# Attention kernel on one core: scores and attention times v in phases per block, with norm and projections spread over blocks

## The chip, the cores and the metric

The kernel runs on one core of a Trainium2 chip. TensorE (PE) multiplies matrices into PSUM, ScalarE (ACT) evaluates functions, VectorE (DVE) and GpSimd (POOL) do elementwise work, SyncE (SP) issues the DMAs. The metric is the device time of one execution in microseconds (us), the median of several runs.

## The reference

The input x has the shape 16 x 256 x 32 x 32. Two layers of the same form follow one another; each adds to x an attention over the 1024 positions of an image, with four heads of 64 channels. All in float32.

```python
def layer(x, Wq, bq, Wk, bk, Wv, bv, rel_h, rel_w):        # x: 16, 256, 32, 32
    xf = gn(x).reshape(16, 256, 1024)     # gn: mean and variance over the channels, the first
                                          # space axis and pairs of the last axis: 16 groups
    q, k, v = (W @ xf + b, each as 16, 4, 64, 1024)
    rel  = (rel_h + rel_w).reshape(4, 64, 1024)
    attn = softmax(einsum('bhdi,bhdj->bhij', q, k) + einsum('hdi,bhdj->bhij', rel, q), -1)
    return x + einsum('bhdn,bhmn->bhdm', v, attn).reshape(x.shape)
```

## The kernel before

The work is cut into 32 *units*: one image in one layer. The images alternate, so that layer 1 of an image comes three units after its layer 0 (for the first image two). A unit has four *blocks*: two pairs of heads (pr), and for each two halves of 512 rows i. A block has eight *chunks* j of 128 columns of the softmax axis. The tiles of a block carry pr and half in their names: `ps_0_1_2` is the score tile of pair 0, half 1, chunk 2; the last number in the order listings only tells buffers apart.

`scores` makes one chunk for both heads of the pair: per head k times q, and two matmuls that add the position term from its two parts `hi` and `lo`. The head of 64 channels takes half of the rows of the array. The scores lie in a PSUM tile `ps`, of which there are three; every projection (`pq`, `pk`, `pv`), the position term `pa`, the group means `pm` and the denominators `pd` take tiles of the same three. ACT writes p = exp(ps - 36) to SBUF, and DVE adds the p of the eight chunks into `acc`. `attend` multiplies two chunks of p with v into `po`, half of the columns of the array per head; `po` lies in one of two PSUM tiles for the whole block.

The denominators (`denominators`): a matmul of acc with ones gives `pd`, ACT copies it to SBUF (`den`), and two DMAs put it across the partitions (`den_all`), so that DVE takes the reciprocal of 8 numbers per partition (L284). A DMA writes these to DRAM (`rd`), another reads them back, repeated for all partitions of a head (`rden`). I call this the trip. `finish` multiplies `po` by `rden` (L298) and adds bias and x (L299); in layer 1 an image's half is then written out (L301).

The work for the next unit is cut into slices, of which one goes behind each chunk from the second block on: the norm (DVE sums, PE averages over partitions, POOL subtracts, squares, takes the power -0.5 and multiplies: L128 to L140), and then the projections. `attend` follows two chunks behind the scores. The denominators of a block come behind the fourth chunk of the next block, and finish behind the eighth.

The order on each engine is not quite that of the text: a scheduler takes the instructions by their place in the text and by when it expects their operands and buffers, and lays down one list per engine, which the engine then works off in order.

## Time and profile before

| | |
|---|---|
| time, median of 3 runs | 3864.93 us (3862.89 to 3867.33) |
| profiled execution | 3863.41 us, span 3861.6 us |
| granted TensorE clock, mean over the span | 0.963 of 2.4 GHz |
| PE busy | 3538.8 us, 92% |
| PE weight loads (beside matmuls) | 1501.0 us, 39% |
| DVE busy | 1705.3 us, 44% |
| ACT busy | 1490.2 us, 39% |
| POOL busy | 676.1 us, 18% |
| DMA traffic | 72.33 MB, 19 GB/s |

A row of the groups by line shows: line, engine, operation, output <- inputs by the program's names, shapes, count | busy us in total, mean ns of one | idle us of the engine just before them, and what ended it. A row of a timeline shows: start in us, length in us, engine, line, operation, output <- inputs, number of instructions merged, and in brackets the idle time before it and what released it. A matmul in float32 shows as two instructions per operand pair; lengths of successive matmuls overlap, so the time that one costs is read from start to start. A row of the windows shows: window in us and its length, then busy us (and count) of PE, PE's weight loads, DVE, ACT and POOL, the granted clock, the share of the DMA engines' time and GB/s.

### The profile page before, as it was taken

How to read it: one execution, taken by the hardware profiler on the slowest of the kernel's cores; microseconds unless marked ns; L12 is line 12 of the kernel's file. 1: busy time of each engine (PE TensorE's matmuls, PEld its weight loads, DVE VectorE, ACT ScalarE, POOL GpSimd, SP SyncE). 2: the span in 40 equal slices, each digit the busy share in tenths (PEclk: the TensorE clock that was granted, in tenths of full speed). 3: DMA queues.
4: the chain of work that ended last, by engine and by line, in shares of the span. 5: the costliest groups of instructions: out<-in, count | busy, mean ns of one | idle time of the engine just before them, and what ended most of it. 6: DMA issues, size and time to landing. Idle time of an engine off the chain costs nothing.

```text
span 3861.6 us, 37025 instructions
## 1 busy us (share of the span) xinstructions
PE 3538.8 (92%) x15386; PEld 1501.0 (39%) x15386; DVE 1705.3 (44%) x1556; ACT 1490.2 (39%) x1409; POOL 676.1 (18%) x134
## 2 busy tenths in 40 slices
PE   6999999999989999999999989999999999999996
PEld 3433443334433334333344333443333433334432
DVE  2444444444434444344543344433355444454443
ACT  2333443344433344333344333443343433334433
POOL 2122111221112221122211122111222112221110
PEclk9999999999999999999999999999999999999998
DMA  1000000000000000000000000000000000000000
GB/s 51 9 9 17 25 9 14 27 16 26 9 15 27 15 27 8 17 25 15 28 9 31 9 15 27 9 31 9 17 25 11 29 11 15 25 18 14 9 15 31
DMA packets 69487, 72.33 MB, mean 19 GB/s; under 512 B 43200, under 2 KB 44736, under 8 KB 69312
## 3 DMA queue, kind: packets, MB, share of 16 engines
q1 hardware_dynamic: 69312, 69.90, 5.3%
q8 instruction: 122, 2.00, 0.2%
q14 instruction: 53, 0.43, 0.0%
HBM read 52.04 MB, written 17.30 MB: 18 GB/s over the span
## 4 chain that ended last, share of the span: by engine, by line
PE 53%; POOL 16%; DMA 16%; DVE 12%; issue 2%; SPq 1%; ACT 1%; DVEq 0%; POOLq 0%
PE ps L233 12%; DMA rden<-rd 12%; PE po L257 11%; PE pq L152 7%; PE pv L196 6%; PE pk L152 6%; PE ps L238 5%; POOL xc L128 4%; POOL rstd L139 4%; DVE acc L248 4%; POOL xc L140 4%; POOL sq L130 4%; PE pa L170 3%; DMA rd<-r 3%; DMA den_all<-den 2%; PE pd L276 2%
## 5 line engine op out<-in xcount | busy, mean ns | idle before, releaser
L242 ACT ACTIVATE p<-ps,shift 128x1024 f32<-128x1024 f32 x1024 | 1141.4, 1115 | 1006.3 <-PE ps L238 996.4
L248 DVE TENSOR_TENSOR acc<-acc,p 128x1024 f32<-128x1024 f32 x768 | 1121.0, 1460 | 603.5 <-ACT p L242 574.2
L257 PE MATMUL po<-p,v 128*64 128x512 f32 x4096 | 1036.2, 628 | 123.1 <-DVE o L298 123.1
L233 PE MATMUL ps<-q,k 64*128 64x512 f32 x4096 | 1132.2, 629 | 0.0
L238 PE MATMUL ps<-pick,hi 64*128 64x512 f32 x2048 | 826.4, 800 | 0.0
L128 POOL TENSOR_TENSOR xc<-x,mean 128x2048 f32<-128x2048 f32 x32 | 175.7, 5491 | 2432.9 <-DVE mean L126 2432.9
L233 PEld LDWEIGHTS ps<-q,k 64*128 64x128 f32 x4096 | 341.9, 187 | 493.4 <-issue 335.1
L257 PEld LDWEIGHTS po<-p,v 128*64 128x64 f32 x4096 | 255.4, 139 | 622.5 <-issue 479.2
L238 PE MATMUL ps<-pick,lo 64*128 64x512 f32 x2048 | 411.0, 393 | 0.0
L298 DVE TENSOR_TENSOR o<-po,rden 128x512 f32<-128x512 f32 x128 | 88.6, 692 | 701.4 <-DMA rden<-rd 656.0
L152 PE MATMUL pq<-xc,Wq 128*128 128x512 f32 x512 | 271.7, 680 | 108.0 <-POOL xc L140 108.0
L139 POOL TENSOR_TENSOR rstd<-var,mhalf 128x32 f32<-128x32 f32 x32 | 204.9, 6405 | 584.5 <-DVE var L135 584.5
L238 PEld LDWEIGHTS ps<-pick,hi 64*128 64x128 f32 x2048 | 200.3, 189 | 245.9 <-issue 245.9
L238 PEld LDWEIGHTS ps<-pick,lo 64*128 64x128 f32 x2048 | 199.7, 188 | 244.8 <-issue 244.8
L280 ACT COPY den<-pd 128x512 f32<-128x512 f32 x128 | 75.1, 587 | 437.6 <-PE pd L276 436.0
L196 PE MATMUL pv<-Wv,xc 128*128 128x256 f32 x1024 | 237.8, 385 | 0.0
L152 PE MATMUL pk<-xc,Wk 128*128 128x512 f32 x512 | 236.6, 605 | 0.0
L246 DVE TENSOR_TENSOR acc<-p,p 128x1024 f32<-128x1024 f32 x128 | 156.4, 1222 | 128.5 <-ACT p L242 128.5
L196 PEld LDWEIGHTS pv<-Wv,xc 128*128 128x128 f32 x1024 | 189.4, 190 | 60.2 <-ACT p L242 25.2
L152 PEld LDWEIGHTS pq<-xc,Wq 128*128 128x128 f32 x512 | 104.4, 214 | 260.5 <-issue 138.8
L180 DVE TENSOR_TENSOR lo<-pa,hi 128x1024 fp32r<-128x1024 f32 x64 | 78.4, 1224 | 283.2 <-ACT hi L179 282.8
L160 ACT ACTIVATE q<-pq,bq 128x1024 f32<-128x1024 f32 x64 | 71.3, 1115 | 340.2 <-PE pq L152 340.2
(57 smaller groups left out, 1322.6 us busy)
## 6 DMA issues: line engine op xcount, KB each, us to landing
rden<-rd SPq DMA_DIRECT2D x128, 256.0 KB
x<-in_x_dram SPq DMA_DIRECT2D x32, 512.0 KB
out_dram<-x SPq DMA_DIRECT2D x32, 512.0 KB
den_all<-den SPq DMA_DIRECT2D x256, 2.0 KB
rd<-r SPq DMA_DIRECT2D x128, 4.0 KB
wn0Wq<-in_L_conv_Wq_dram SPq DMA_DIRECT2D x1, 256.0 KB
wn0Wk<-in_L_conv_Wk_dram SPq DMA_DIRECT2D x1, 256.0 KB
wn0Wv<-in_L_conv_Wv_dram SPq DMA_DIRECT2D x1, 256.0 KB
```

The lines of the kernel that those rows point to most:

```text
L128: nc.gpsimd.tensor_tensor(rows(xc, H), rows(src, H), per_column(mean), ALU.subtract)
L130: nc.gpsimd.tensor_tensor(sq, xc, xc, ALU.mult)
L139: nc.gpsimd.tensor_tensor(rstd, var, W.mhalf, ALU.pow)
L140: nc.gpsimd.tensor_tensor(rows(xc, H), rows(xc, H), per_column(rstd), ALU.mult)
L152: nc.tensor.matmul(pk[:, nh, :], w[l][:, cc, pr * P : (pr + 1) * P], xns[u][:, cc, nh * HALF : (nh + 1) * HALF], start=(cc == 0), stop=(cc ...
L196: nc.tensor.matmul(pv[:, i, :], xns[u][:, cc, t * P : (t + 1) * P], W.wv[l][:, cc, :], start=(cc == 0), stop=(cc == CC - 1),)
L233: nc.tensor.matmul(ps[:, h, :], ks[u, pr][hs[h], jc], qs[u, pr][hs[h], ic], start=True, stop=False)
L238: nc.tensor.matmul(ps[:, h, :], part[u, pr][hs[h], jc], W.pick[hs[h], ic], start=False, stop=last)
L242: nc.scalar.activation(p, ps, AF.Exp, bias=W.shift)
L246: nc.vector.tensor_tensor(accs[blk], probs[blk, 0], p, ALU.add)
L248: nc.vector.tensor_tensor(accs[blk], accs[blk], p, ALU.add)
L257: nc.tensor.matmul(outs[blk][h * D : (h + 1) * D, :], vts[u][:, j, c0 : c0 + D], p[:, h, :], start=(j == 0), stop=(j == NT - 1),)
```

## The change

`attend` now runs once per block, over all eight chunks, and makes `pd` right behind; both `po` and `pd` take tiles of the pool of two, and ACT copies both to SBUF. `reciprocals` is the rest of the trip; it stands behind the fourth chunk of the next block, and `finish`, which reads the copy of po, behind the eighth. The norm is cut in four pieces and the projections in three groups, each at a fixed place: `before_block` runs ahead of the scores of a block, `norm_a` and `norm_c` behind them. The variance's power is taken on 16 columns instead of 32, and POOL spreads the result with a copy. The projections of q and k for the first pair of heads come a block early, in the last block of the unit before. There are 3 instead of 4 buffers for each of q, k, hi and lo, and 10 instead of 8 for p.

```diff
-    kqpool = ctx.enter_context(tc.tile_pool(name="kqpool", bufs=4))
+    kqpool = ctx.enter_context(tc.tile_pool(name="kqpool", bufs=3))
-    ppool = ctx.enter_context(tc.tile_pool(name="ppool", bufs=8))
+    ppool = ctx.enter_context(tc.tile_pool(name="ppool", bufs=10))
...
+    def norm_d(u):
+        xc = xns[u]
+        var = small.tile([P, G], F32, tag="var", name=f"var_{u}")
+        nc.vector.tensor_scalar(var, group_mean(u, "v"), EPS, None, ALU.add)
+        rstd = small.tile([P, G], F32, tag="rstd", name=f"rstd_{u}")
+        nc.gpsimd.tensor_tensor(rstd, var, W.mhalf[:, :G], ALU.pow)
+        rs = small.tile([P, H], F32, tag="rs", name=f"rs_{u}")
+        nc.gpsimd.tensor_copy(rs.rearrange("p (g t) -> p g t", t=GT), spread(rstd))
+        nc.gpsimd.tensor_tensor(rows(xc, H), rows(xc, H), per_column(rs), ALU.mult)
...
-    def attend(blk, j):
+    def attend(blk):
...
+        po = ps_o.tile([P, HALF], F32, tag="o", name=f"po_{name}")
+        for j in range(NT):
...
+        pd = ps_o.tile([P, HALF], F32, tag="o", name=f"pd_{name}")
...
+        outs[blk] = fpool.tile([P, HALF], F32, tag="ou", name=f"ou_{name}")
+        nc.scalar.copy(outs[blk], po)
...
-        o = fpool.tile([P, HALF], F32, tag="o", name=f"o_{u}_{pr}_{half}")
-        nc.vector.tensor_tensor(o, outs.pop(blk), rdens.pop(blk), ALU.mult)
+        o = outs.pop(blk)
+        nc.vector.tensor_tensor(o, o, rdens.pop(blk), ALU.mult)
...
+    def before_block(n):
+
+        u, b = divmod(n, BPU)
+        nxt = u + 1 if u + 1 < len(units) else None
+        if b == 0:
+            if u > 0:
+                positions(u, 0)
+            values(u, 0)
+            values(u, 1)
+        elif b == 1:
+            if nxt is not None:
+                norm_b(nxt)
+            project(u, 1, "q")
+            project(u, 1, "k")
+            positions(u, 1)
+        elif b == 2:
+            if nxt is not None:
+                norm_d(nxt)
+        elif nxt is not None:
+            project(nxt, 0, "q")
+            project(nxt, 0, "k")
...
+    for n, blk in enumerate(blocks):
+        before_block(n)
+        for j in range(NT):
+            scores(blk, j)
+            if n > 0 and j == 3:
+                reciprocals(blocks[n - 1])
+        if n > 0:
             finish(blocks[n - 1])
...
+            if b == 0:
+                norm_a(u + 1)
+                if u + 2 < len(units) and units[u + 2][1] == 0 and units[u + 2][0] > 1:
+                    load_x(units[u + 2][0])
+            elif b == 1:
+                norm_c(u + 1)
+        attend(blk)
```

PE, the end of the second block of unit 4, before (`ps` are scores, `po` attention times v):

```order
L233 MATMUL ps_0_1_6_2646<-q_0_2247,k_0_2271 128x512 x2
L238 MATMUL ps_0_1_6_2646<-pick,hi_0_2285 128x512 x2
L238 MATMUL ps_0_1_6_2646<-pick,lo_0_2286 128x512 x2
L233 MATMUL ps_0_1_7_2656<-q_0_2247,k_0_2271 128x512 x2
L238 MATMUL ps_0_1_7_2656<-pick,hi_0_2285 128x512 x2
L238 MATMUL ps_0_1_7_2656<-pick,lo_0_2286 128x512 x2
L257 MATMUL po_0_1_2604<-p_0_1_4_2629,v_2304 64x512 x2
L257 MATMUL po_0_1_2604<-p_0_1_5_2639,v_2304 64x512 x2
L233 MATMUL ps_1_0_0_2676<-q_1_2368,k_1_2385 128x512 x2
L238 MATMUL ps_1_0_0_2676<-pick,hi_1_2404 128x512 x2
```

and now, where the eight rows of po stand together, of which the first and the last are shown, and `pd` and the variance's `pm_v` follow:

```order
L231 MATMUL ps_0_1_7_2675<-q_0_2301,k_0_2308 128x512 x2
L236 MATMUL ps_0_1_7_2675<-pick,hi_0_2427 128x512 x2
L236 MATMUL ps_0_1_7_2675<-pick,lo_0_2428 128x512 x2
L257 MATMUL po_0_1_2690<-p_0_1_0_2606,v_2431 64x512 x2
...
L257 MATMUL po_0_1_2690<-p_0_1_7_2682,v_2431 64x512 x2
L267 MATMUL pd_0_1_2707<-acc_0_1_2617,ones 64x512 x2
L121 MATMUL pm_v_2717<-red_v_2687,avg 128x16 x2
L231 MATMUL ps_1_0_0_2726<-q_1_2583,k_1_2590 128x512 x2
```

Two chunks of scores and two of po took turns; now eight and eight do, with one change of form each way.

DVE in the second block of unit 4, before. `r_4_0_0` is the reciprocal for the block before it, `o` and `x` are the two operations of its finish, `red_v` sums the squares that POOL makes from `xc`:

```order
L246 TENSOR_TENSOR acc_0_1_2569<-p_0_1_0_2555,p_0_1_1_2567 128x1024
L126 COPY mean_2588<-pm_m_2585 128x32
L248 TENSOR_TENSOR acc_0_1_2569<-acc_0_1_2569,p_0_1_2_2582 128x1024
L248 TENSOR_TENSOR acc_0_1_2569<-acc_0_1_2569,p_0_1_3_2601 128x1024
L104 TENSOR_REDUCE red_v_2673<-sq_2592 128x16 x2
L104 TENSOR_REDUCE red_m_3100<-x_935 128x16 x2
L284 RECIPROCAL r_4_0_0_2616<-den_all 128x8
L248 TENSOR_TENSOR acc_0_1_2569<-acc_0_1_2569,p_0_1_4_2629 128x1024
L248 TENSOR_TENSOR acc_0_1_2569<-acc_0_1_2569,p_0_1_5_2639 128x1024
L298 TENSOR_TENSOR o_0_0_2670<-po_0_0_2479,rden_0_0_2620 128x512
L299 SCALAR_TENSOR_TENSOR x_206<-o_0_0_2670,bv_156,x_206 128x512
L248 TENSOR_TENSOR acc_0_1_2569<-acc_0_1_2569,p_0_1_6_2653 128x1024
```

and now, from the mean on, where `ou` is the copy of po, and `lo_1` is the second part of the position term of the next pair of heads:

```order
L140 COPY mean_2569<-pm_m_2570 128x32
L284 RECIPROCAL r_4_0_0_2639<-den_all 128x8
L109 TENSOR_REDUCE red_v_2687<-sq_2576 128x16 x2
L296 TENSOR_TENSOR ou_0_0_2563<-ou_0_0_2563,rden_0_0_2643 128x512
L297 SCALAR_TENSOR_TENSOR x_206<-ou_0_0_2563,bv_156,x_206 128x512
L196 TENSOR_TENSOR lo_1_2596<-pa_1_2592,hi_1_2595 128x1024
L244 TENSOR_TENSOR acc_0_1_2617<-p_0_1_0_2606,p_0_1_1_2615 128x1024
L246 TENSOR_TENSOR acc_0_1_2617<-acc_0_1_2617,p_0_1_2_2626 128x1024
```

The reciprocal and both operations of finish have moved ahead of all additions of the block, and so have red_v and lo_1.

DVE in the first block of unit 5, before:

```order
L246 TENSOR_TENSOR acc_0_0_2992<-p_0_0_0_2981,p_0_0_1_2990 128x1024
L248 TENSOR_TENSOR acc_0_0_2992<-acc_0_0_2992,p_0_0_2_3005 128x1024
L248 TENSOR_TENSOR acc_0_0_2992<-acc_0_0_2992,p_0_0_3_3015 128x1024
L284 RECIPROCAL r_4_1_1_3030<-den_all 128x8
L248 TENSOR_TENSOR acc_0_0_2992<-acc_0_0_2992,p_0_0_4_3043 128x1024
L248 TENSOR_TENSOR acc_0_0_2992<-acc_0_0_2992,p_0_0_5_3053 128x1024
L298 TENSOR_TENSOR o_1_1_3084<-po_1_1_2884,rden_1_1_3034 128x512
L299 SCALAR_TENSOR_TENSOR x_206<-o_1_1_3084,bv_156,x_206 128x512
L248 TENSOR_TENSOR acc_0_0_2992<-acc_0_0_2992,p_0_0_6_3067 128x1024
```

and now, where `x_3089` is the tile of an image that this block loads, for the norm of unit 7:

```order
L196 TENSOR_TENSOR lo_0_2973<-pa_0_2969,hi_0_2972 128x1024
L284 RECIPROCAL r_4_1_1_3037<-den_all 128x8
L296 TENSOR_TENSOR ou_1_1_2963<-ou_1_1_2963,rden_1_1_3041 128x512
L297 SCALAR_TENSOR_TENSOR x_206<-ou_1_1_2963,bv_156,x_206 128x512
L244 TENSOR_TENSOR acc_0_0_3015<-p_0_0_0_3004,p_0_0_1_3013 128x1024
L109 TENSOR_REDUCE red_m_3633<-x_3089 128x16
L246 TENSOR_TENSOR acc_0_0_3015<-acc_0_0_3015,p_0_0_2_3024 128x1024
L109 TENSOR_REDUCE red_m_3633<-x_3089 128x16
L246 TENSOR_TENSOR acc_0_0_3015<-acc_0_0_3015,p_0_0_3_3034 128x1024
```

The reciprocal and finish stand ahead of the first addition, and the two sums of the new image between the first additions. In the third block the same two operations follow the first addition; in the fourth they stand ahead of all.

## Rows read from the trace of the kernel before

**Rows 1.** Groups of instructions by line, six lines out of all
```profile
L257 PE MATMUL po<-p,v 128*64 128x512 f32 x4096 | 1036.2, 628 | 123.1 <-DVE o L298 123.1
...
L152 PE MATMUL pq<-xc,Wq 128*128 128x512 f32 x512 | 271.7, 680 | 108.0 <-POOL xc L140 108.0
...
L139 POOL TENSOR_TENSOR rstd<-var,mhalf 128x32 f32<-128x32 f32 x32 | 204.9, 6405 | 584.5 <-DVE var L135 584.5
...
L140 POOL TENSOR_TENSOR xc<-xc,rstd 128x2048 f32<-128x2048 f32 x32 | 152.8, 4774 | 2.5
...
L280 ACT COPY den<-pd 128x512 f32<-128x512 f32 x128 | 75.1, 587 | 437.6 <-PE pd L276 436.0 <-DMA x<-in_x_dram 1.6
...
L114 PE MATMUL pm_m<-red_m,avg 128*128 128x16 f32 x128 | 20.4, 271 | 6.2 <-DVE red_m L104 6.2
```

**Rows 2.** Timeline of PE, one undisturbed pair and two pauses
```profile
1016.76 1.94 PE L257 MATMUL po<-p,v 128*64 128x512 f32 x8
...
1089.15 5.40 PE L152 MATMUL pq<-xc,Wq 128*128 128x512 f32 x8 [3.90 <-POOL xc L140]
...
2857.37 2.84 PE L257 MATMUL po<-p,v 128*64 128x512 f32 x8 [2.92 <-DVE o L298]
```

**Rows 3.** Timeline of PE at the start
```profile
51.10 3.60 PE L152 MATMUL pk<-xc,Wk 128*128 128x512 f32 x8
54.53 1.88 PE L170 MATMUL pa<-q,rel 128*128 128x512 f32 x4
56.25 7.07 PE L196 MATMUL pv<-Wv,xc 128*128 128x256 f32 x32
...
71.83 1.13 PE L233 MATMUL ps<-q,k 64*128 64x512 f32 x4
...
73.27 1.02 PE L233 MATMUL ps<-q,k 64*128 64x512 f32 x4
...
74.58 1.03 PE L233 MATMUL ps<-q,k 64*128 64x512 f32 x4
```

**Rows 4.** Timeline of all engines, the last block
```profile
3825.59 3.65 PE L257 MATMUL po<-p,v 128*64 128x512 f32 x16
...
3834.26 1.81 PE L276 MATMUL pd<-acc,ones 128*64 128x512 f32 x4 [5.01 <-DVE acc L248]
...
3839.07 0.20 DVE L284 RECIPROCAL r<-den_all 128x8 f32<-128x8 f32 x1 [4.96 <-DMA den_all<-den]
...
3848.07 0.69 DVE L298 TENSOR_TENSOR o<-po,rden 128x512 f32<-128x512 f32 x1 [8.80 <-DMA rden<-rd]
```

**Rows 5.** Timeline of PE and DVE, the longest trip to DRAM
```profile
403.44 1.03 PE L276 MATMUL pd<-acc,ones 128*64 128x512 f32 x4
...
418.32 0.69 DVE L298 TENSOR_TENSOR o<-po,rden 128x512 f32<-128x512 f32 x1 [6.29 <-DMA rden<-rd]
```

**Rows 6.** Timeline of DVE, mid-run
```profile
1134.07 0.69 DVE L298 TENSOR_TENSOR o<-po,rden 128x512 f32<-128x512 f32 x1 [5.01 <-DMA rden<-rd]
...
1135.47 1.22 DVE L248 TENSOR_TENSOR acc<-acc,p 128x1024 f32<-128x1024 f32 x1
1136.67 1.23 DVE L180 TENSOR_TENSOR lo<-pa,hi 128x1024 fp32r<-128x1024 f32 x1
...
1167.96 0.18 DVE L126 COPY mean<-pm_m 128x32 f32<-128x32 f32 x1
...
1169.54 5.32 DVE L248 TENSOR_TENSOR acc<-acc,p 128x1024 f32<-128x1024 f32 x1 [0.16 <-ACT p L242]
1178.35 2.35 DVE L104 TENSOR_REDUCE red_v<-sq 128x16 f32<-128x1024 f32 x2 [3.49 <-POOL sq L130]
```

**Rows 7.** Timeline of the SP queue, a write of x and the next load
```profile
1164.47 0.34 SPq L301 DMA_DIRECT2D out_dram<-x  x1
1167.49 0.82 SPq L86 DMA_DIRECT2D x<-in_x_dram  x2
```

**Rows 8.** Busy time by window, the end of that load
```profile
1171.00:1171.50 0.50, 0.50 (x4) 0.30 (x4) 0.50 (x1) 0.38 (x1) 0.50 (x1) 1.00 0.63 254
```

More of the change, by code (lines that the diff above doesn't have):

```diff
@@ L66, in fast_path @@
     NL = sh.NL
-    LAG = 2
     xpool = ctx.enter_context(tc.tile_pool(name="xpool", bufs=3))
@@ L99, in psum2, with reduce_groups @@
         return ps_s.tile([P, 2, HALF], F32, tag="s", name=name)
-    def group_mean(src, name):
-        red = small.tile([P, CC, G], F32, tag="red", name=f"red_{name}")
+    reds = {}
+    def reduce_groups(u, src, what):
+        red = small.tile([P, CC, G], F32, tag=f"red_{what}", name=f"red_{what}_{u}")
         for cc in range(CC):
@@ L109, in group_mean @@
             )
-        yield
-        yield
-        pm = psum2(f"pm_{name}")
+        reds[u, what] = red
+    def group_mean(u, what):
+        red = reds.pop((u, what))
+        pm = psum2(f"pm_{what}_{u}")
         for cc in range(CC):
@@ L130, in norm_slices, with norm_c @@
         nc.gpsimd.tensor_tensor(sq, xc, xc, ALU.mult)
-        for _ in range(5):
-            yield
-        pv = yield from group_mean(sq, f"v{u}")
-        var = small.tile([P, H], F32, tag="var", name=f"var_{u}")
-        nc.vector.tensor_scalar(
-            var.rearrange("p (g t) -> p g t", t=GT), pv, EPS, None, ALU.add
-        )
-        rstd = small.tile([P, H], F32, tag="rstd", name=f"rstd_{u}")
-        nc.gpsimd.tensor_tensor(rstd, var, W.mhalf, ALU.pow)
-        nc.gpsimd.tensor_tensor(rows(xc, H), rows(xc, H), per_column(rstd), ALU.mult)
-        xns[u] = xc
-        for _ in range(5):
-            yield
+        xns[u], sqs[u] = xc, sq
+    def norm_c(u):
+        reduce_groups(u, sqs.pop(u), "v")
+    def norm_d(u):
[7 more added lines that the diff above has]
+        nc.gpsimd.tensor_tensor(rows(xc, H), rows(xc, H), per_column(rs), ALU.mult)
     def project(u, pr, which):
@@ L301, in finish @@
             nc.sync.dma_start(flat(out[b, pr * P : (pr + 1) * P]), xt[b][:, pr, :])
-    for f in (norm_slices, projection_slices):
-        for _ in f(0):
-            pass
     blocks = [(u, pr, half) for u in range(len(units)) for pr in range(CC) for half in range(NH)]
@@ L310, in fast_path @@
         index[blk] = n
-    steps = [(blk, j) for blk in blocks for j in range(NT)]
-    BPU = CC * NH * NT
-    prep = iter(())
-    for g in range(len(steps) + LAG):
-        if g < len(steps):
-            scores(*steps[g])
-        if g % 2 == 1:
-            for a in (g - LAG - 1, g - LAG):
-                if 0 <= a < len(steps):
-                    attend(*steps[a])
-        n, c = divmod(g, NT)
-        if c == LAG + 1 and n > 0:
-            rdens[blocks[n - 1]] = denominators(blocks[n - 1])
-        if c == NT - 1 and n > 0:
+    BPU = CC * NH
+    def before_block(n):
[18 more added lines that the diff above has]
+            project(nxt, 0, "k")
+    for f in (norm_a, norm_b, norm_c, norm_d):
+        f(0)
+    project(0, 0, "q")
+    project(0, 0, "k")
+    positions(0, 0)
+    for n, blk in enumerate(blocks):
[5 more added lines that the diff above has]
+        if n > 0:
             finish(blocks[n - 1])
-        u, step = divmod(g, BPU)
-        if g < len(steps):
-            if step == NT:
+        u, b = divmod(n, BPU)
+        if u + 1 < len(units):
+            if b == 0:
+                norm_a(u + 1)
                 if u + 2 < len(units) and units[u + 2][1] == 0 and units[u + 2][0] > 1:
                     load_x(units[u + 2][0])
-                if u + 1 < len(units):
-                    prep = chain(norm_slices(u + 1), projection_slices(u + 1))
-            next(prep, None)
-    blk = blocks[-1]
-    for a in range(len(steps) - LAG, len(steps)):
-        if (steps[a][0], steps[a][1]) in probs:
-            attend(*steps[a])
-    rdens[blk] = denominators(blk)
-    finish(blk)
+            elif b == 1:
+                norm_c(u + 1)
+        attend(blk)
+    reciprocals(blocks[-1])
+    finish(blocks[-1])
 @with_exitstack
```

75 lines of the change are left out of this document (28 added, 47 removed).

## The prediction

> **What bounds the kernel now.** I read the share of each engine first, then the list of groups by line, then the timelines of PE, DVE and SP around one unit, and last how the change orders PE and DVE. PE is the engine that is busy nearly all the time; what it loses are drains and two pauses in each unit. In the list of groups [rows 1] the reader is to see the idle time ahead of two lines: 123.1 us before attention times v (L257), which waits for DVE's product o because o still holds the PSUM tile, and 108.0 us before the q projection (L152), which waits for POOL's normalised xc. The PE timeline shows what these pauses also do to the clock [rows 2]: after 3.90 us of pause eight projection matmuls take 5.40 us, against 3.60 us for the same eight in [rows 3]; after 2.92 us eight matmuls of po take 2.84 instead of 1.94 us. I read both as stretches at the lower of the clock's two levels, 1.2 instead of 2.4 GHz, behind a pause. I take the first one's 5.40 - 3.60 = 1.8 us per pause of two to four us.
>
> A unit of before takes (3836.07 - 71.83) / 32 = 117.6 us, from the first score [rows 3] to the end of the last pd [rows 4].
>
> **The change on PE.** The matmuls are the same; what goes are switches between forms. At the start, where four chunks of scores stand in a row, the first lasts 1.44 us to the start of the next and the second 1.31 [rows 3]; so eight chunks take 1.44 + 7 x 1.31 = 10.61 us. Attention times v for two chunks lasts 1.94 us, for four 3.65 [rows 2, 4], so each further pair 1.71 and all eight 1.94 + 3 x 1.71 = 7.07. pd takes 1.03 [rows 5]; q or k 3.43 and pa 1.72 from start to start, both halves of v 7.07 [rows 3]; a group mean 20.4 / 32 = 0.64 [rows 1]. At full clock, without waits:
> - first block (pa, v): 1.72 + 7.07 + 10.61 + 7.07 + 1.03 = 27.5 us
> - second (mean, q, k, pa): 0.64 + 3.43 + 3.43 + 1.72 + 18.71 = 27.9 us
> - third (variance): 0.64 + 18.71 = 19.35 us
> - fourth (next q, k): 6.86 + 18.71 = 25.6 us
>
> Together 100.35 us. If that were all, the change would take off a seventh.
>
> **The change on DVE.** Here the order decides. In the text the reciprocal follows the fourth chunk and finish the eighth; in DVE's queue both stand ahead of nearly all additions of the block, and everything behind waits for the reciprocal's trip through DRAM. I count from T, the end of the preceding block's pd. The last block of before shows the trip undisturbed: pd ends at 3836.07, the reciprocal starts 3.00 us later, the product 12.00 us later [rows 4]. The longest trip that I found lasts 418.32 - 404.47 = 13.85 us [rows 5]. I take 12.0, and keep 13.85 for the range. Product and addition to x take 1.40 us, an addition 1.22, lo 1.23 [rows 6].
>
> Third block: the variance, the reciprocal and the first addition are done early. The product comes at T + 12.0, six additions end at 12.0 + 1.4 + 6 x 1.22 = 20.7, while PE wants pd at 0.64 + 10.61 + 7.07 = 18.3. PE waits 2.4 us.
>
> Second block: the reduce of sq stands ahead of the product, and lo behind it. The mean starts at T + 0.74; the reduce starts 10.39 us after the mean, since POOL makes xc and sq in between, and takes 2.35 [rows 6], so it ends at 13.5; product and x end at 14.9, lo at 16.1. The third chunk of scores needs the PSUM tile that lo reads: with three tiles, the mean's goes to pa, and pa's to this chunk. PE is there at 9.22 + 1.44 + 1.31 = 12.0 and waits 4.1 us. The additions end well before pd.
>
> Fourth block: the additions end at 12.0 + 1.4 + 7 x 1.22 = 21.9; PE comes at 24.5. No wait, 2.6 us of cover. First block: lo comes first, behind pa (1.72) and ACT's cast of pa (a us, estimated from den's copy of half the size, 0.587 [rows 1]); so the reciprocal starts at 4.0 and the product, 9.0 behind it [rows 4], at 13.0; with one reduce of x the additions end at 24.1, and PE comes at 26.5. The cover is 2.4 us.
>
> Thirteen units (every odd one from 3 to 27) are heavier. Their first block has two reduces of an x that is only then loaded, among the additions. The load waits for the write of the x before it in its buffer: SP issues it 3.02 us after that write [rows 7], and its transfer ends 4.0 us after the issue [rows 8]. So: finish ends at T + 14.4, load issued at 17.4, halves there at about 20.0 and 21.4 (half of the megabyte each), reduce, addition, reduce, five additions end at 29.7. PE waits 3.2 us. Their third block has one reduce more: 21.9 instead of 20.7, and PE waits 3.6.
>
> **Other edits.** The copy of po is like den's, 0.587 us [rows 1]; ACT makes it while PE does pd, so it costs nothing; wholly in the way it would add 0.6 us to the trip. It frees PSUM early, and the 123.1 us go. The pow on half the columns and the new copy on POOL lie between nothing (pow at zero) and 6.4 us for the pow, with the multiplication's 4.8 behind it [rows 1]; even with a us for the copy xc is ready by T + 13 of the third block, and the q projection that wants it comes at T + 21.7. So the 108.0 us go as well. Fewer buffers for q and k and more for p: by the order nothing waits for them.
>
> The product now reads two operands in SBUF. The Trainium skill (SBUF — State Buffer, Who interferes with whom) says that a VectorE instruction with two SBUF inputs contends with a GpSimd instruction that reads SBUF, and that the one that starts second is held for all of the other. The trace agrees for an addition beside POOL's xc: 5.32 us instead of 1.22 [rows 6]. By that rule the product of the third block, beside POOL's multiplication, could be held to T + 13 at the latest, which adds up to 1 us to that block; by the forecast it is not held, since the multiplication ends before T + 12.
>
> **The sum.** A light unit: 100.35 + 4.1 + 2.4 + 2 x 1.8 = 110.5 us. A heavy one: 100.35 + 4.1 + 3.6 + 3.2 + 3.6 + 1.0 = 115.9 us; the last 1.0 is its pd at half clock, and the rest of that fall lies under the next wait. Start to the first score: 71.83 - 3.43 - 3.43 - 1.72 = 63.2. First unit: 110.5 - 8.8 (pa and v are in the start) = 101.7. Then 17 light units 1878.5 and 13 heavy ones 1506.7. Last unit, without a norm: lo ends at 14.6, and its third and fourth block end with the additions and pd at 21.7: 27.5 + 30.6 + 21.7 + 21.7 + three falls 5.4 = 107. End as before, 3861.6 - 3836.1 = 25.5. Sum 3682.6 us of span. The profiled execution of before took 1.8 us more than its span, and the median of the runs 1.5 us more than it: 3686 us, 4.6% less.
>
> **Rivals.**
> - The reciprocal is held by POOL. In the second block it falls beside xc. No row has it there. An addition that came late beside xc could begin only 5.68 us after the mean (1169.54 + 5.32 - 1.22 - 1167.96, [rows 6]). Then it starts at T + 6.4, the product at 15.4, lo ends at 18.0: 1.9 us more in 31 units, 3746 us. For it: additions are held. Against it: it has one small operand. The page of the Trainium skill named above says that an instruction with at most one SBUF input, outside the two-port modes, is not held; by it this rival falls; no row can show it.
> - The clock stays up after these waits, which are mostly shorter than 4 us: 18 x 3.6 + 13 x 4.6 + 5 = 130 us less, 3556 us. Against it: the row after 2.92 us.
> - The phases do not bring what I read: every chunk costs 1.44 and every pair of po 1.87. That is 1.3 us a block where PE sets the end: about 3.7 us in a light and 2.4 in a heavy unit, 98 us, 3784 us. Against it: the second and third chunk of [rows 3].
> - The waits in DVE's queue are all covered: 100.35 us a unit, 3286 us. Against it: the trip's 12.0 us, and the end of before [rows 4], where pd already sits 5.01 us behind such a product.
> - Slower: DVE's queue becomes the loop that sets the time, because the trip lasts longer where each block starts one. Four us more (16.0) cost 1.7 + 2.5 + 4.0 + 1.4 us in the blocks of a light unit and two further falls of the clock, 13.2 us, and 13.7 in a heavy one: 415 us, 4101 us. It decides from 2.8 us more (14.8) on, where the 5.8 us that a unit has gained are gone. For it: one trip of 13.85 us. Against it: the chain has no new step but the copy.
>
> **How the numbers follow.** Forecast 0.56; reciprocal held 0.17; clock up 0.08; phases without gain 0.05; all covered 0.03; trip longer 0.11. The forecast's own range is 3670 to 3780: a trip of 13.85 us costs some 92 us, and downwards half of the falls behind the 2.4 us waits may stay out (18 x 1.8 / 2 = 16 us). The range of 3550 to 3800 takes in the reciprocal, the clock and the phases, and leaves out the last two. About 0.2% is what a measurement can tell from no change. All cases but the long trip are faster by more: 0.89; of the long trip 0.02 falls near its turning point, and 0.09 is slower.
>
> **What would show it.** Right: PE's longest waits are for lo ahead of the third chunk in the second block, about 4 us, 31 times, and for the additions ahead of pd in the third block, 2 to 4 us, and in 13 first blocks; DVE's longest total is the product's wait for rden, 7 to 9 us each; a score chunk in a row takes 1.31 us; no pause before po or before the next unit's q. Wrong: pauses in first or fourth blocks of light units (a longer trip), a reciprocal that ends with xc, matmuls at full clock behind the waits, or chunks of 1.4 us.

## The result, and the profile after

The changed kernel takes 3642.28 us in the median of four runs (3635.63 to 3650.66), the one before took 3863.91 us beside it (3855.39 to 3867.33): ratio 0.9431, interval 0.9403 to 0.9458. The forecast was 3686 us, in a range of 3550 to 3800. The profiled execution took 3650.66 us, its span 3648.8 us, at a mean granted clock of 0.959.

The groups by line of the kernel after, which answer to [rows 1]; the columns are the same:

```profile
L231 PE MATMUL ps<-q,k 64*128 64x512 f32 x4096 | 1077.8, 601 | 57.2 <-DVE lo L196 57.2
...
L257 PE MATMUL po<-p,v 128*64 128x512 f32 x4096 | 907.1, 595 | 0.0
...
L168 PE MATMUL pq<-xc,Wq 128*128 128x512 f32 x512 | 308.8, 758 | 8.1 <-POOL xc L158 8.1
...
L267 PE MATMUL pd<-acc,ones 128*64 128x512 f32 x512 | 163.8, 724 | 177.8 <-DVE acc L246 177.8
...
L142 POOL TENSOR_TENSOR xc<-x,mean 128x2048 f32<-128x2048 f32 x32 | 144.3, 4510 | 2250.9 <-DVE mean L140 2250.9
...
L144 POOL TENSOR_TENSOR sq<-xc 128x2048 f32<-128x2048 f32 x32 | 115.2, 3599 | 2.5
...
L155 POOL TENSOR_TENSOR rstd<-var,mhalf 128x16 f32<-128x16 f32 x32 | 92.8, 2900 | 710.6 <-DVE var L153 710.6
L296 DVE TENSOR_TENSOR ou<-ou,rden 128x512 f32<-128x512 f32 x128 | 88.6, 692 | 666.8 <-DMA rden<-rd 640.4 <-ACT p L240 26.2
```

Both old pauses are gone: nothing is idle ahead of po (L257; 123.1 us before), and 8.1 us ahead of q (L168; 108.0 before), which is the very first normalisation. po takes 907.1 us of PE in place of 1036.2. Two new waits stand in their place: 57.2 us ahead of scores (L231), for lo, and 177.8 us ahead of pd (L267), for the additions. DVE's idle time ahead of the product (L296), until rden has come, is 640.4 us, 5.0 us each on average: 8.7 us in first and fourth blocks, 2.5 in third and 0.5 in second ones, where the prediction's sign had 7 to 9 us each.

PE in a light unit, second and third block, with the third chunk of scores at 2120.00:

```profile
2116.15 1.04 PE L231 MATMUL ps<-q,k 64*128 64x512 f32 x4
...
2120.00 1.13 PE L231 MATMUL ps<-q,k 64*128 64x512 f32 x4 [2.34 <-DVE lo L196]
...
2147.32 7.09 PE L257 MATMUL po<-p,v 128*64 128x512 f32 x32
2157.75 1.08 PE L267 MATMUL pd<-acc,ones 128*64 128x512 f32 x4 [3.34 <-DVE acc L246]
2158.76 3.70 PE L168 MATMUL pq<-xc,Wq 128*128 128x512 f32 x8
```

DVE in the same two blocks:

```profile
2106.16 0.19 DVE L140 COPY mean<-pm_m 128x32 f32<-128x32 f32 x1 [3.13 <-PE pm_m L121]
2108.65 0.20 DVE L284 RECIPROCAL r<-den_all 128x8 f32<-128x8 f32 x1 [2.30 <-DMA den_all<-den]
2114.67 2.35 DVE L109 TENSOR_REDUCE red_v<-sq 128x16 f32<-128x1024 f32 x2 [5.81 <-POOL sq L144]
2117.33 0.69 DVE L296 TENSOR_TENSOR ou<-ou,rden 128x512 f32<-128x512 f32 x1 [0.32 <-DMA rden<-rd]
...
2118.73 1.22 DVE L196 TENSOR_TENSOR lo<-pa,hi 128x1024 fp32r<-128x1024 f32 x1
...
2140.66 5.16 DVE L244 TENSOR_TENSOR acc<-p,p 128x1024 f32<-128x1024 f32 x1 [1.30 <-ACT p L240]
2148.43 0.69 DVE L296 TENSOR_TENSOR ou<-ou,rden 128x512 f32<-128x512 f32 x1 [2.62 <-DMA rden<-rd]
...
2149.83 7.87 DVE L246 TENSOR_TENSOR acc<-acc,p 128x1024 f32<-128x1024 f32 x6
```

In the second block lo begins when the sums of sq, the product and the addition to x have ended, and PE waits 2.34 us for it. In the third block six additions stand behind the product, which waits for rden until 2148.43, and PE waits 3.34 us for the last; the first addition, which takes 5.16 us beside POOL's multiplication, was done before. The reciprocal takes 0.20 us at 2108.65, though POOL makes xc beside it:

```profile
2106.43 4.53 POOL L142 TENSOR_TENSOR xc<-x,mean 128x2048 f32<-128x2048 f32 x1 [70.37 <-DVE mean L140]
2111.04 3.60 POOL L144 TENSOR_TENSOR sq<-xc 128x2048 f32<-128x2048 f32 x1
...
2140.17 4.56 POOL L158 TENSOR_TENSOR xc<-xc,rs 128x2048 f32<-128x2048 f32 x1
```

A heavy first block, DVE, with the new image's sums (`red_m`) waiting 5.08 us for its transfer:

```profile
2197.67 0.69 DVE L296 TENSOR_TENSOR ou<-ou,rden 128x512 f32<-128x512 f32 x1 [8.80 <-DMA rden<-rd]
...
2205.37 1.22 DVE L109 TENSOR_REDUCE red_m<-x 128x16 f32<-128x1024 f32 x1 [5.08 <-DMA x<-in_x_dram]
...
2207.91 1.22 DVE L109 TENSOR_REDUCE red_m<-x 128x16 f32<-128x1024 f32 x1 [0.19 <-DMA x<-in_x_dram]
2209.05 6.53 DVE L246 TENSOR_TENSOR acc<-acc,p 128x1024 f32<-128x1024 f32 x5
```

PE behind it, and busy time in three windows: behind the wait for lo of the light unit, the end of the heavy block's wait, and q behind that (the number after POOL's is the granted clock):

```profile
2215.63 1.97 PE L267 MATMUL pd<-acc,ones 128*64 128x512 f32 x4 [4.49 <-DVE acc L246]
...
2218.41 6.56 PE L168 MATMUL pq<-xc,Wq 128*128 128x512 f32 x8
2224.81 3.60 PE L168 MATMUL pk<-xc,Wk 128*128 128x512 f32 x8
```

```profile
2120.00:2123.00 3.00, 3.00 (x18) 1.84 (x20) 1.30 (x2) 1.12 (x1) 0.00 (x0) 1.00 0.00 0
2211.20:2215.60 4.40, 0.00 (x0) 0.00 (x0) 4.07 (x4) 0.57 (x1) 0.00 (x0) 0.82 0.00 0
2219.00:2224.00 5.00, 5.00 (x7) 2.01 (x6) 0.20 (x1) 0.00 (x0) 4.92 (x2) 0.50 0.04 5
```

Behind the 2.34 us for lo the clock is still 1.00; behind the 4.49 us it is 0.50, so 1.2 GHz, and q takes 6.40 us to the start of k instead of 3.52. Waits of such a length do not all end alike: behind the 3.34 us of the third block above, too, the clock is 1.00 and q takes 3.54 us, while over all light units q is 1.31 us longer there on average.

From the end of one pd to the end of the next, means over the 17 light and the 13 heavy units (us):

| block | forecast light | after | forecast heavy | after | kernel with the product last (below) |
|---|---|---|---|---|---|
| first | 27.5 | 27.46 | 31.7 | 32.64 | 27.46 |
| second | 33.8 | 31.43 | 33.8 | 30.79 | 28.69 |
| third | 21.75 | 23.48 | 22.95 | 24.00 | 19.19 |
| fourth | 27.4 | 27.02 | 27.4 | 27.30 | 25.71 |
| unit | 110.5 | 109.39 | 115.9 | 114.73 | 101.07 |

(The forecast's fall of the clock behind a wait is counted in the block in which the slow matmuls stand.)

### The profile page after: what moved, and what is told of

Read it like the earlier page. It is cut to its first block, busy times and chain, and to the rows that moved or that the text cites. A ratio compares the mean times of both kernels' runs of the same rounds, so it can differ in the third digit from the quotient of the medians.

```text
span 3648.8 us, 37268 instructions
## 1 busy us (share of the span) xinstructions
PE 3353.9 (92%) x15386; PEld 1613.8 (44%) x15386; DVE 1661.8 (46%) x1556; ACT 1565.7 (43%) x1537; POOL 505.7 (14%) x166
## 4 chain that ended last, share of the span: by engine, by line
PE 56%; DMA 21%; DVE 13%; issue 6%; POOL 1%; ACT 1%; SPq 1%; DVEq 0%; POOLq 0%
PE po L257 15%; PE ps L231 15%; DMA rden<-rd 13%; DVE acc L246 8%; PE ps L236 8%; PE pq L168 5%; PE pd L267 4%; PE pv L212 4%; PE pk L168 3%; DMA den_all<-den 3%; DMA rd<-r 3%; PE pa L186 2%; DVE x L297 1%; DVE ou L296 1%; DMA x<-in_x_dram 1%
## 5 line engine op out<-in xcount | busy, mean ns | idle before, releaser
L231 PE MATMUL ps<-q,k 64*128 64x512 f32 x4096 | 1077.8, 601 | 57.2 <-DVE lo L196 57.2
L246 DVE TENSOR_TENSOR acc<-acc,p 128x1024 f32<-128x1024 f32 x768 | 940.3, 1224 | 125.7 <-ACT p L240 57.5
L257 PE MATMUL po<-p,v 128*64 128x512 f32 x4096 | 907.1, 595 | 0.0
L257 PEld LDWEIGHTS po<-p,v 128*64 128x64 f32 x4096 | 282.8, 137 | 557.7 <-issue 557.7
L231 PEld LDWEIGHTS ps<-q,k 64*128 64x128 f32 x4096 | 389.4, 186 | 194.6 <-DVE lo L196 69.4
L142 POOL TENSOR_TENSOR xc<-x,mean 128x2048 f32<-128x2048 f32 x32 | 144.3, 4510 | 2250.9 <-DVE mean L140 2250.9
L271 ACT COPY ou<-po 128x512 f32<-128x512 f32 x128 | 75.0, 586 | 756.4 <-PE po L257 756.4
L296 DVE TENSOR_TENSOR ou<-ou,rden 128x512 f32<-128x512 f32 x128 | 88.6, 692 | 666.8 <-DMA rden<-rd 640.4
L267 PE MATMUL pd<-acc,ones 128*64 128x512 f32 x512 | 163.8, 724 | 177.8 <-DVE acc L246 177.8
L168 PE MATMUL pq<-xc,Wq 128*128 128x512 f32 x512 | 308.8, 758 | 8.1 <-POOL xc L158 8.1
L244 DVE TENSOR_TENSOR acc<-p,p 128x1024 f32<-128x1024 f32 x128 | 278.0, 2172 | 61.9 <-ACT p L240 61.8
L168 PE MATMUL pk<-xc,Wk 128*128 128x512 f32 x512 | 230.2, 592 | 0.0
L168 PEld LDWEIGHTS pq<-xc,Wq 128*128 128x128 f32 x512 | 121.3, 250 | 187.0 <-issue 178.0
```

Of the source, the lines that this page charges most:

```text
L142: nc.gpsimd.tensor_tensor(rows(xc, H), rows(src, H), per_column(mean), ALU.subtract)
L168: nc.tensor.matmul(pk[:, nh, :], w[l][:, cc, pr * P : (pr + 1) * P], xns[u][:, cc, nh * HALF : (nh + 1) * HALF], start=(cc == 0), stop=(cc ...
L231: nc.tensor.matmul(ps[:, h, :], ks[u, pr][hs[h], jc], qs[u, pr][hs[h], ic], start=True, stop=False)
L244: nc.vector.tensor_tensor(accs[blk], probs[blk, 0], p, ALU.add)
L246: nc.vector.tensor_tensor(accs[blk], accs[blk], p, ALU.add)
L257: nc.tensor.matmul(po[h * D : (h + 1) * D, :], vts[u][:, j, c0 : c0 + D], p[:, h, :], start=(j == 0), stop=(j == NT - 1),)
```

## The experiments

The theory: what is left of waits comes from one place in DVE's queue, where the product stands until rden has come back from DRAM, with lo and the additions behind it. The rivals: these waits are DVE's and POOL's own work; or the gain came only from the two pauses that went, and the phases did nothing. Ratios are to the kernel before, beside it on the same chip.

### Without the trip, with the trip out of the way, and the load of x

**No trip.**

```diff
-        r8 = fpool.tile([P, 8], F32, tag="r8", name=f"r8_{name}")
-        nc.vector.reciprocal(r8, den_all[:, index[blk], :])
-        rd = dpool.tile([2, HALF], F32, tag="rd", name=f"rd_{name}")
-        nc.sync.dma_start(rd.rearrange("h (a b) -> (h a) b", b=8), r8)
...
-        nc.sync.dma_start(rdens[blk], rd.unsqueeze(1).to_broadcast([2, D, HALF]))
+        nc.vector.reciprocal(rdens[blk], dens.pop(blk))
```

> The kernel after with the reciprocal taken by DVE on den as it lies (128x512), in place of the trip through DRAM; the two copies into den_all stay for the test at the end. Theory (what is left of waits is the product standing in DVE's queue until rden has come, ahead of lo and of the additions): the waits for lo (2.3 us) and for the additions (3.3 us) go with their stretches at the lower clock; a light unit falls from 109.4 to about 101 us, a heavy one from 114.7 to 102 to 106 (its load of x still waits for a write, but of an image that is finished 8 us earlier): 17 x 8.4 + 13 x 11 + 6 = 290 us less, 3350 us. Rival (the waits are DVE's own work and POOL's xc and sq, so that the trip is cover that costs nothing): over 3550 us. Rival (a reciprocal of 512 columns takes several us and stands where the wait stood): 3450 to 3600 us.

Measured: 3383.12 us, ratio 0.8778 (0.8762 to 0.8794). 33 us above what was expected. A light unit takes 102.97 us, a heavy one 104.35. Groups by line, then DVE's timeline, of this kernel:

```profile
L231 PE MATMUL ps<-q,k 64*128 64x512 f32 x4096 | 1068.5, 596 | 47.7 <-DVE lo L196 47.7
...
L285 DVE RECIPROCAL rden<-den 128x512 f32<-128x512 f32 x128 | 428.6, 3348 | 263.4 <-ACT den L273 263.4
...
L267 PE MATMUL pd<-acc,ones 128*64 128x512 f32 x512 | 133.2, 598 | 39.3 <-DVE acc L246 39.3
```

```profile
2052.31 3.34 DVE L285 RECIPROCAL rden<-den 128x512 f32<-128x512 f32 x1
...
2061.05 1.22 DVE L109 TENSOR_REDUCE red_v<-sq 128x16 f32<-128x1024 f32 x1 [3.49 <-POOL sq L144]
...
2063.97 1.21 DVE L196 TENSOR_TENSOR lo<-pa,hi 128x1024 fp32r<-128x1024 f32 x1
...
2086.09 4.93 DVE L294 SCALAR_TENSOR_TENSOR x<-ou,bv,x 128x512 f32<-128x512 f32 x1
```

The rival of cover that costs nothing falls: the two waits shrink from 235.0 to 87.0 us although DVE now has 428.6 us of reciprocals more, and so does the last: the reciprocal takes 3.35 us, but the time stays under the 3450 us that this rival had as its least. What stays is lo behind the sums of sq (1.54 us on average in the second block) and, in the third block, an x that takes 4.93 us beside POOL's multiplication, instead of 0.74; neither was expected to stay.

**Four buffers for x**, with the trip and without it:

```diff
-    xpool = ctx.enter_context(tc.tile_pool(name="xpool", bufs=3))
+    xpool = ctx.enter_context(tc.tile_pool(name="xpool", bufs=4))
```

> The kernel after with four buffers for x in place of three, so that the load of an image in odd first blocks need not wait until the image before it in that buffer has been written out. Theory: the sums of the new x no longer stand in DVE's queue waiting 5 us for the transfer, the additions end before PE wants pd, the first block of the 13 heavy units falls from 32.6 to about 27.8 us, and its slow matmuls behind the wait go; some comes back as the wait for lo in the second block, 2.3 us as in light units in place of 0.6, so 13 x (4.8 - 1.0) = 50 us less, 3590 us. Rival (the product's wait for rden, 8.8 us, decides in these blocks and the load lies beside it): no change, 3642 us.

Measured: 3573.57 us, ratio 0.9276 (0.9257 to 0.9294), 16 us below the expectation. The heavy first block takes 27.46 us instead of 32.64, and its wait is gone; the wait for lo in heavy units comes back, 2.58 us on average, where 2.3 was expected. The forecast's step on the load of x is right.

> The same without the trip, and with four buffers for x. Theory: as without the trip, and the heavy units' wait for the load of x goes as well: every unit near the 100.4 us of PE's work alone, span about 63 + 92 + 30 x 101 + 100 + 15 = 3300 us. Rival (once the trip is gone the load of x comes early enough with three buffers): the same time as without the trip and with three buffers, within 10 us.

Measured: 3408.11 us, ratio 0.884 (0.8825 to 0.8854): slower than with three buffers, against both expectations. PE's waits for lo in two successive second blocks of this kernel:

```profile
310.40 1.13 PE L231 MATMUL ps<-q,k 64*128 64x512 f32 x4 [2.95 <-DVE lo L196]
...
413.23 1.13 PE L231 MATMUL ps<-q,k 64*128 64x512 f32 x4 [1.54 <-DVE lo L196]
```

In every other second block the wait is 2.95 instead of 1.54 us. With a fourth buffer the scheduler takes the sums of the next image earlier: in these blocks one of them stands ahead of the reciprocal and the other, 1.2 us long, right ahead of lo. These thirteen blocks pay 1.4 us of wait more each, and some 0.7 us on average in slower matmuls behind it: 28 us, as much as the two spans differ (3405.3 and 3377.7). The heavy first blocks, which the fourth buffer was to help, have no wait without the trip in either kernel. More room moved an instruction to a worse place.

**The trip kept, the product behind the last addition** (and four buffers for x). The product gets one factor more, a 1 that is made from the last column of the block's sum, so that it can't stand ahead of the last addition:

```diff
-        nc.vector.tensor_tensor(o, o, rdens.pop(blk), ALU.mult)
+            one = small.tile([P, 1], F32, tag="one", name=f"one_{u}_{pr}_{half}")
+            nc.vector.tensor_scalar(one, accs[after][:, 1, HALF - 1 : HALF], 0.0, 1.0, ALU.mult, ALU.add)
+            nc.vector.scalar_tensor_tensor(o, o, one, rdens.pop(blk), ALU.mult, ALU.mult)
...
-            finish(blocks[n - 1])
+            finish(blocks[n - 1], blk)
```

> The kernel after with four buffers for x, and with the trip through DRAM kept, but the product forced behind the block's last addition in DVE's queue: it takes a factor of 1 that is made from that addition's result. Theory (the trip's length costs nothing; its place in DVE's queue, ahead of lo and the additions, costs all): the waits for lo and for the additions go as they did without the trip, the second block keeps the 1.5 us that POOL's sq costs there, a unit about 102 us in place of 108 to 110 with four buffers for x alone: 3575 - 30 x 7 = 3360 us, ratio 0.87. Rival (the trip itself is needed sooner than the end of a block, so that the wait comes back for ou's or rden's buffers or for x): 3500 us or more, ratio 0.91. Rival (additions that now stand beside POOL's xc and sq hold each other): 3420 to 3500 us.

Measured: 3304.82 us, ratio 0.8544 (0.853 to 0.8558), 55 us below what was expected, with all its transfers through DRAM. Its groups, and DVE at the end of a block:

```profile
L231 PE MATMUL ps<-q,k 64*128 64x512 f32 x4096 | 1067.8, 596 | 16.8 <-DVE lo L196 16.8
...
L168 PE MATMUL pq<-xc,Wq 128*128 128x512 f32 x512 | 238.6, 609 | 8.1 <-POOL xc L158 8.1
...
L301 DVE SCALAR_TENSOR_TENSOR ou<-ou,one,rden 128x512 f32<-128x512 f32 x127 | 95.5, 752 | 5.1 <-DVE one L300 0.6
```

```profile
2096.24 0.15 DVE L300 TENSOR_SCALAR one<-acc 128x1 f32<-128x1 f32 x1
2096.43 0.75 DVE L301 SCALAR_TENSOR_TENSOR ou<-ou,one,rden 128x512 f32<-128x512 f32 x1
2097.22 0.75 DVE L302 SCALAR_TENSOR_TENSOR x<-ou,bv,x 128x512 f32<-128x512 f32 x1
```

The product no longer waits for rden but in the very last block, no wait for pd is left, and 16.8 us for lo. Beside the kernel with the same four buffers (3573.57 us, ratio 0.9276) some 270 us go, with every step of the trip still there: not the trip's length but the product's place in DVE's queue made these waits. Against the kernel after, and so for the two edits together, the account closes: spans 3648.8 - 3302.8 = 346.0 us; waits 57.2 + 177.8 - 16.8 = 218.2, and PE busy 3353.9 - 3226.4 = 127.5 us for the same matmuls at a higher clock (0.959 to 0.997), together 345.7. The Trainium skill (DMA: Bandwidth & Descriptors, Rules for kernel authors) says to issue a DMA early, compute, and wait on its semaphore late; the trace agrees, with these 270 us.

The first rival is right for a part of the wait for lo. Of its 2.80 us in light second blocks of the kernel after, DVE's waiting for rden is 0.78 us on average; the product and the addition to x, which are work ahead of lo, take 1.40; and the 0.55 that stays with the product last is behind the sums of sq.

**The norm one block earlier**, without the trip, three buffers for x. In this kernel the last unit's mean is summed before the last block of that image's layer 0 is added to x (for the last image, as for the first, layer 1 comes two units after layer 0). It leaves that block out of the mean, so its output for the last image is not that of the reference; it is a measurement of the order, not a kernel to use.

```diff
+            if nxt is not None and nxt != 2:
+                norm_b(nxt)
             values(u, 0)
             values(u, 1)
         elif b == 1:
...
+            elif nxt is not None:
+                norm_d(nxt)
...
+            elif b == 3 and u > 0 and u + 2 < len(units):
+                norm_a(u + 2)
```

> The kernel after without the trip (three buffers for x), and with the norm of the next unit begun one block earlier: the sums of x in the fourth block of the unit before, mean, xc and sq in the first block, variance, power and multiplication in the second (for the third unit as before). Theory: without the trip, what is left of waits is 1.5 us for lo behind the sums of sq in the second block and 1.8 us for the additions in the third, behind a product and x held beside POOL's multiplication, and the heavy units' load; in the first and second block there is room for each, so a unit comes to the 100.4 us of PE's work: 3383 - 17 x 2.5 - 13 x 4 = 3290 us, ratio 0.853. Rival (the same waits appear in the first block, where DVE now has the sums of sq ahead of all additions): 3380 us or more, ratio 0.878.

Measured: 3301.35 us, ratio 0.8537 (0.8522 to 0.8553). The wait for lo is gone but for one of 1.55 us; 19.7 us for the additions are left in heavy first blocks, 1.5 us each, which the expected 3290 us did not have. The rival, 3380 us or more, falls. A light unit takes 100.46 us, where the forecast's sum of PE's work alone is 100.35.

### The phases

**Pairs again:**

```diff
+            if j in (3, 5, 7):
+                attend_part(blk, j - 3, j - 1)
```

> The kernel after, but attention times v goes in pairs of chunks between the scores again (behind chunks 4, 6 and 8, and the rest at the end); the early copy of po, the placed norm and the order of the rest stay. Theory (eight matmul rows of one form in a row save the switches): three more changes of form each way per block cost 3 x (1.44 - 1.31) + 3 x (1.94 - 1.71) = 1.1 us wherever PE sets the end of a block, which is first, second and fourth block of a light unit and second and fourth of a heavy one; in third blocks and heavy first blocks PE merely waits 1.1 us less for the additions. 17 x 3.3 + 13 x 2.2 + 5 = 90 us more than after, 3730 us. Rival (the gain of the change was only the two pauses that went, po's tile and q's normalised input; form switches cost nothing): within 10 us of after, 3642 us. Rival (finer turns let the additions end earlier relative to PE, the waits shrink by more than the switches cost): below 3620 us.

Measured: 3703.01 us, ratio 0.96 (0.9584 to 0.9616), against 0.9431 in phases; 61 us more and not 90. PE in a block of it:

```profile
2164.49 1.94 PE L260 MATMUL po<-p,v 128*64 128x512 f32 x8
2166.35 1.13 PE L231 MATMUL ps<-q,k 64*128 64x512 f32 x4
```

The expectation counted three changes of form more; there are two, since the third pair stands next to the rest. A light first block, which has no wait in either kernel, takes 28.18 instead of 27.46 us: 0.72 us, twice the 0.13 + 0.23 = 0.36 us of a change each way. The rival without gain falls, and so does the one of shrinking waits. Heavy units stay as they were (114.69 and 114.73): their waits for the additions shrink by 1.0 us in first and 0.6 in third blocks, and the slow matmuls behind the latter by 1.5 us, which makes up for the switches. The Trainium skill (TensorEngine Tiling (Array Packing), Key Properties) says that changing the tiling mode drains TensorE; the trace agrees in that a change there and back costs PE 0.36 us.

Switches are not all of the 61 us. A light second block takes 33.79 us instead of 31.43: besides 0.72 for two turns and 0.2 of longer wait for lo, the matmuls behind that wait are 1.4 us slower. In one of them, behind 2.37 us of wait, the granted clock from 2141.70 to 2144.40 is 0.50, where it was 1.00 behind the 2.34 us above; over 17 light units that is 24 us. Why the clock falls here and not there, no run shows.

### Parts of the change on the kernel before

**The copy of po alone, the power on 16 columns alone, both, and the phases alone.** Their cores:

```diff
+        if j == NT - 1:
+            ou = fpool.tile([P, HALF], F32, tag="ou", name=f"ou_{u}_{pr}_{half}")
+            nc.scalar.copy(ou, outs[blk])
+            outs[blk] = ou
```
```diff
+        rs = small.tile([P, G], F32, tag="rs", name=f"rs_{u}")
+        nc.gpsimd.tensor_tensor(rs, var, W.mhalf[:, :G], ALU.pow)
```
```diff
+        if g % NT == NT - 1 and g < len(steps):
+            for a in range(g - NT + 1, g + 1):
+                attend(*steps[a])
```

> The kernel before with one part of the change: ACT copies po to SBUF behind its last chunk, and finish works on the copy. Theory: po's PSUM tile is free early, the 123.1 us ahead of po in [rows 1] go, and with each of these some 42 pauses of 2.9 us the 0.9 us of slow matmuls behind it [rows 2]: 160 us less than before, ratio 0.958. Rival (PE merely meets the same DVE queue a little later, at pd or at q's projection): ratio above 0.985. Rival (phases are the whole gain of the change): 1.00.

> The kernel before with another part of the change: the power -0.5 on 16 columns, spread by a copy on POOL. Theory: POOL's normalised xc comes 3.3 us earlier (6.4 us become 2.9 and 0.2), which takes the 3.4 us (108.0 / 32) ahead of q's projection away and with it the 1.8 us of the fall behind: 32 x 5.1 = 160 us less than before, ratio 0.958. Rival (the pause is set by the chain ahead of the power, DVE's var and PE's mean, and only the power's share of it goes without the fall): ratio 0.972 to 0.98. Rival (none of it on the path): 1.00.

> Both of these parts on the kernel before: the copy of po and the power on 16 columns; the order of the chunks stays as before. Theory (the two pauses are independent, and the order of before covers the trip through DRAM since lo and the additions don't stand behind it): both gains add up, 320 us less, ratio 0.917, which would be faster than the changed kernel. Rival (one pause hides the other): ratio 0.94 to 0.96, no better than the change.

> The kernel before with the phases alone: attention times v for all eight chunks behind the eighth chunk of scores, without the copy of po, the norm and projections left in their slices. Theory: 1.1 us less for switches in each of 128 blocks, 140 us; and po now lives only from the end of a block to finish in the next, so that its pause, 123.1 us and the slow matmuls behind it, goes without a copy too: 300 us less, ratio 0.92, while the 108.0 us ahead of q's projection stay. Rival (the phases bring additions and finish late against PE as in the kernel after, with new waits of 9 us a unit): ratio 0.96 to 1.0.

| | us | ratio | interval |
|---|---|---|---|
| copy | 3840.41 | 0.9926 | 0.9901 to 0.9951 |
| power | 3769.33 | 0.9746 | 0.972 to 0.9771 |
| both | 3762.82 | 0.9722 | 0.9695 to 0.9748 |
| phases | 3776.76 | 0.9764 | 0.9741 to 0.9788 |

The theories expected far more of each. The copy came out as its first rival had it: above 0.985, with the wait at pd. The power's ratio is in the range of its first rival, though not for the rival's reason: the pause ahead of q falls by 64.3 us, and the slow q behind it goes as well (271.7 us to 241.4), together 94.6 of the 95 us. The phases' ratio is in their rival's range, but by a wait for var, not for the additions. Both parts together fit neither forecast. One group by line of the copy, one of the power, one of the phases:

```profile
L280 PE MATMUL pd<-acc,ones 128*64 128x512 f32 x512 | 160.9, 712 | 204.1 <-DVE var L135 199.2 <-DVE acc L248 5.0
```

```profile
L158 PE MATMUL pq<-xc,Wq 128*128 128x512 f32 x512 | 241.4, 615 | 43.7 <-POOL xc L146 43.7
```

```profile
L233 PE MATMUL ps<-q,k 64*128 64x512 f32 x4096 | 1134.7, 631 | 185.7 <-DVE var L135 185.7
```

The pause ahead of po is gone with the copy, but 199.2 us stand ahead of pd, for var, where it was 34.5 in the kernel before; in the phases 185.7 us ahead of the next scores, for var too. DVE and PE of the kernel with both parts show why:

```profile
1045.78 0.69 DVE L308 TENSOR_TENSOR ou<-ou,rden 128x512 f32<-128x512 f32 x1 [6.58 <-DMA rden<-rd]
...
1050.77 0.17 DVE L138 TENSOR_SCALAR var<-pm_v 128x16 f32<-128x16 f32 x1
```

```profile
1050.99 1.98 PE L286 MATMUL pd<-acc,ones 128*64 128x512 f32 x4 [6.36 <-DVE var L138]
```

var reads a PSUM tile that pd wants, and stands in DVE's queue behind the product, which waits 6.58 us for rden. It is the same wait under a third name. So the parts aren't worth what the pauses ahead of them show: 2.5% the power, 2.4% the phases, 0.7% the copy; the whole change 5.7%. The whole change also puts var ahead of the product (var comes 0.6 us behind pd in the third block) and pd on another pool, and no wait of PE for var is left in its groups; that these two keep the wait away fits, but was not tried by itself.

**The kernel before without the trip:**

```diff
-        nc.vector.reciprocal(r8, den_all[:, n, :])
...
+        nc.vector.reciprocal(rden, den)
```

> The kernel before with the reciprocal taken by DVE on den as it lies (128x512), without the trip, nothing else. Theory (the same wait, the product at the head of DVE's queue until rden has come, makes most of the pauses of before too: po's tile, var behind it, and by var the power and the late xc): 123 us and 38 of slow matmuls behind them, 35 of pd's wait for var, and some of the 108 ahead of q: 200 to 260 us less, ratio 0.94. Rival (the pauses of before come from the order of PE's work and from POOL's power, not from the trip): ratio 0.98 or more.

Measured: 3720.41 us, ratio 0.9614 (0.9596 to 0.9631): more than the theory's 0.94, less than the rival's 0.98, so neither. No pause ahead of po is left, but q's grew from 108.0 us, and pd's wait for var, which the theory had going, from 34.5:

```profile
L152 PE MATMUL pq<-xc,Wq 128*128 128x512 f32 x512 | 303.7, 748 | 131.0 <-POOL xc L140 131.0
...
L276 PE MATMUL pd<-acc,ones 128*64 128x512 f32 x512 | 133.0, 598 | 50.2 <-DVE var L135 50.2
```

Why both grew I have not taken apart. q's pause is 43.7 us with the power on 16 columns (above) and 8.4 with the copy as well, but it does not go with the trip. Without the trip in either kernel the change is worth more than with it: from ratio 0.9614 to 0.8778, in place of 1 to 0.9431.

**The kernel after with the power on 32 columns:**

```diff
-        nc.gpsimd.tensor_tensor(rstd, var, W.mhalf[:, :G], ALU.pow)
-        rs = small.tile([P, H], F32, tag="rs", name=f"rs_{u}")
-        nc.gpsimd.tensor_copy(rs.rearrange("p (g t) -> p g t", t=GT), spread(rstd))
+        nc.gpsimd.tensor_tensor(rs, var, W.mhalf, ALU.pow)
```

> The kernel after with the power -0.5 on 32 columns as before, without POOL's spreading copy. Theory (in the kernel after the norm is placed early enough, xc has 8 us to spare ahead of q's projection): the same time, 3642 us within 10, ratio 0.943. Rival (xc is still on the path): 3.3 us in each of 31 units and falls of the clock, 100 to 150 us more, ratio 0.97 to 0.98.

Measured: 3663.12 us, ratio 0.9475 (0.9455 to 0.9496) against 0.9431 (0.9403 to 0.9458). The rival falls: ahead of q 10.4 us are idle in place of 8.1. The placing of the norm had covered the power already. But 21 us more is twice the 10 us that the theory allowed, and the two intervals barely touch. The 0.4% I have not taken apart; light units are 0.1 us longer, heavy ones 0.4, the first unit 4.3.

## Why the prediction was right, step by step

- **PE's work alone** (27.5, 27.9, 19.35, 25.6): right within 0.25 us a block. With the product last the blocks take 27.46, 28.69 less 0.54 of wait, 19.19 and 25.71.
- **The two pauses go, through copy and placing**: right in the kernel after. That the copy frees PSUM "and the 123.1 us go" is true of po, but by the copy alone they come back ahead of pd, for var.
- **Second block, the wait for lo, 4.1 us**: right in mechanism, mis-sized. The step "the reduce starts 10.39 us after the mean" took POOL's xc and sq from [rows 6], where an addition stood beside them. After, no addition does: xc takes 4.51 us and sq 3.60, the reduce starts 8.51 us after the mean, and the light units wait 2.80 us on average. So the sums of sq end at T + 11.4 (13.5 forecast), and the product comes at T + 12.2 on average, when rden is there. In heavy ones, slow q matmuls behind the first block's wait cover it: 0.3 us on average over all 13.
- **Fall of the clock, 1.8 us behind each wait**: 1.9 us behind the light third block's wait (pd 0.58 and q 1.31 longer), but 0.5 behind lo. Behind the heavy first block it is 3.3, in pd, the mean's matmuls and q. In sum 127.5 us, where the forecast had 130: that the two are so near is luck, one error against another.
- **Third block, 2.4 us**: 3.54 measured. The product came at T + 12.35 and not 12.0 in the block shown (12.45 on average), and six additions of one acc take 7.87 us, 1.31 each, where I took the 1.22 of one.
- **Heavy first block, 3.2 us**: 4.17 measured. The load was issued at T + 17.36 (17.4), but its halves were summed at T + 20.83 and T + 23.37, not 20.0 and 21.4; the additions ended at T + 31.0 (29.7).
- **The sum**: second blocks 17 x 2.4 + 13 x 3.0 = 80 us too long; third and fourth blocks 17 x 1.35 + 13 x 0.95 = 35 and heavy first blocks 13 x 0.94 = 12 us too short; 33 us too long in all, and the span is 3682.6 - 3648.8 = 33.8 us shorter. So the mechanism was right, and part of the nearness of the number is luck: errors of 80 and 47 us stand against each other.
- **Rivals**: the reciprocal was not held (0.20 us beside xc). By the rule of the Trainium skill that was named there (SBUF — State Buffer, Who interferes with whom) it should not be; the trace agrees. The trip lengthened little: the product comes at T + 12.1 in fourth blocks and 12.45 in light third ones, where 12.0 was forecast. The clock stays up, as the second rival has it, behind 12 of the 17 waits for lo in light units (1.00 over the 5 us behind them) and falls behind the other five. Phases without gain are wrong: with pairs again a light first block is 0.72 us longer. The waits all covered, 3286 us, is what two further edits (the product last, four buffers for x) come near: 3304.82.
